# A norm's sums behind the next shared products, its square root one iteration later, and image loads in another order

## The chip, the cores and the metric

The kernel runs on one core of a Trainium2 chip. The metric is the device time of one execution in microseconds; several executions give a median and a range. Engines are written as in the profile: PE is TensorE, DVE is VectorE, ACT is ScalarE, POOL is GpSimd, SP is SyncE (here it only issues DMAs).

## The reference

Four residual layers act on x of shape (4, 32, 32, 16): batch, rows, columns, channels. Before each layer stands a group norm with 8 groups. Three layers are a convolution with a kernel of its own for every output pixel; the change lies in these. The fourth, a two-dimensional recursive filter done by Fourier transforms, is not touched.

```
def layer(v, M, W, G):                  # v = _gn(x)
    first   = einsum('ijpq,bpqc->bijc', M, v)
    shifted = conv3x3(v, K from G)       # for each output pixel (i, j): all (p, q), 16 channels
    diff    = relu(v[:, :, :, None, None, :] - shifted)
    second  = einsum('ijpq,bpqijc->bijc', W, diff)
    return first - second
x = x + layer(_gn(x), ...)               # three times

def _gn(v, G=8, eps=1e-5):               # mean and variance over rows, columns and the group's 2 channels
    return (g - m) / sqrt(s + eps)
```

## The kernel before, in words

**The tiles.** The 1024 output pixels of a layer make 128 blocks of 8 pixels by 16 channels, 128 rows of PE's output. One iteration is one block of one batch: PE makes shifted for all 1024 input pixels in a pair of PSUM banks (128 x 1024), and one DVE instruction (L771, 1.22 us) takes the min with zero, multiplies by W and sums along the row. There are 128 x 4 x 3 = 1536 iterations. `order` lists them, from `passes`: at a layer's ends the batches go in pairs, a = 0 (batches 0, 1) and a = 1 (batches 2, 3), so that one pair's norm runs beside the other pair's last blocks.

**One iteration** (`iteration`, L758 to L780). Four PSUM slots rotate. For iteration i PE holds, in its order, the six shared products of iteration i+1 (`shared_products`, L720: the products that two neighbouring pixels have in common, in half of the columns; ACT copies them into the other half, L729), then the own products of iteration i (`own_products`, L749: 16 matmul instructions in the trace, eight with f, the fp32 part of the image, and eight with n, its fp32r part). The products accumulate without a start flag onto columns that ACT has set to zero (`prepare`, L678, which for iteration i+2 is issued in the middle of the own products; `full` marks the slots whose columns were all written, so that this is allowed). The first 24 iterations go another way (`direct`, L701).

**What runs beside.** After each iteration `step()` advances a list of generators by one `yield`: first `todo` (norm, then store, then loads of a pair's image), then `tasks` (loads and splits of the taps, weights W). A `yield` thus is one iteration's distance, and what is issued between two of them takes its place in each engine's queue behind that iteration. The engines' queues are in the order of the program.

**The norm of a pair** (`group_norm`, L187). Row statistics on DVE, split into a high and a low fp32r piece (`in_pieces`); `piece_sums` (L155) adds them over partitions on PE with the matrix avg_r: a matmul with zeros over a whole bank (L165, start flag) and a small one with the pieces (L172), per half; ACT copies the result out (`held`, L181). The second sum is of the squared deviations; DVE then makes the variance v (L229), ACT its root r (L232), DVE refines r. Five norms of a pair go this way (two behind layer 0, two behind layer 1, one behind layer 2), with two sums each. The kernel's other norms use another sum.

**The image.** `store_image` (L401) makes the nine kinds of differences of the normed pair: POOL's subtractions L410, ACT's roundings L411 and L413, POOL's L417, edge copies on POOL (L420) and ACT (L421); then three DMAs on POOL's queue write them to `img` in DRAM (L423 to L425). Four iterations later `load_image` (L429) issues, per batch, 14 DMAs (L458) alternately on SP's and POOL's queue: six pieces of f (16 or 96 KB) and eight of n (72 KB). The second batch's follow three iterations behind the first's. SP's queue also carries the taps g (L588, 1536 KB), W (L634, 1024 KB) and F (L532); POOL splits the taps (L567, L569) and stores them to `gd` (L573).

Of the kernel before, what the change touches and what calls it, by code (L numbers as in the profile page):

```python
# [15 lines left out]
P = 128  # L16
# [21 lines left out]
def conv_stack_kernel(ctx, tc, x, M, W, raw_f, first_g, F, E, h0, coef, cst, dft, idp, idq, out):  # L38
    nc = tc.nc
# [15 lines left out]
    full, banks = [False] * 4, [0]  # L55

    def pair_psum(stays_full=False):
        slot = banks[0] % 4
        banks[0] += 1
        if not stays_full:  # L60
            full[slot] = False
        return ps.tile([P, 2, 512], F32, tag=f"pt{slot}", name="pt")

    def next_psum(stays_full=False):
        pt = pair_psum(stays_full)
        banks[0] -= 1
        return pt
# [14 lines left out]
    avg_r = const.tile([P, P], F32R, name="avg_r")  # L82
# [4 lines left out]
    nought_r = const.tile([P, 2], F32R, name="nought_r")  # L87
    nought = nought_r.bitcast(F32)[:, :1]
# [13 lines left out]
    start = [[range(layer * NBLK + lo, layer * NBLK + hi) for lo, hi in spans[layer]] for layer in range(3)]  # L102
# [20 lines left out]
    now = {"at": 0}  # L123
# [22 lines left out]
    def in_pieces(s):  # L146
# [5 lines left out]
        nc.vector.tensor_tensor(lo, s, hi.bitcast(F32), ALU.subtract)  # L152
        return pieces

    def piece_sums(pieces):  # L155

        pt = next_psum(True)  # L160
        nb, _, nw = pieces.shape[1:]
        n = nb * 4 * nw
        for h in range(2):
            rows = slice(64 * h, 64 * h + 64)
            nc.tensor.matmul(  # L165
                pt[:, h],
                lhsT=avg_r[rows],
                rhs=nought_r[rows].unsqueeze(1).to_broadcast([64, 256, 2]),
                start=True,
                stop=False,  # L170
            )
            nc.tensor.matmul(  # L172
                pt[:, h, :n],
                lhsT=avg_r[rows],
                rhs=pieces[rows].rearrange("p b k w -> p (b k w)"),
                start=False,
                stop=True,
            )
        full[banks[0] % 4] = True
        held = work.tile([P, 2, 16], F32, tag="yt", name="held")[:, :, :n]  # L180
        nc.scalar.copy(held, pt[:, :, :n])  # L181
        return held.rearrange("p h (b k w) -> p b w h k", k=4, w=nw), AX.XY

    def as_it_is(s):
        return s

    def group_norm(xt, operand=in_pieces, sums=piece_sums):  # L187


        nb = xt.shape[1]  # L190
        vec = lambda name, n=1: small.tile([P, 2 * B, n], F32, tag=name, name=name)[:, :out]

        st = small.tile([P, B, 2, 3], F32, tag="st", name="st")[:, :nb]
        for b in range(nb):
            nc.vector.bn_stats(st[:, b].rearrange("p e k -> p (e k)"), xt[:, b])
            if operand is in_pieces:
                yield
        to_add = operand(st[:, :, :, 1:])
        yield
        yield  # L200
        pm, axes = sums(to_add)
        spread = sums is piece_sums
        if spread:
            yield
        out = pm.shape[1]
        both = vec("both", 2)
        nc.vector.tensor_reduce(both, pm, axes, ALU.add)
        neg, within = both[:, :, 0], both[:, :, 1]
        d = vec("d", 2)[:, :nb]
        nc.vector.tensor_tensor(  # L210
            d, st[:, :, :, 1], neg[:, :nb].unsqueeze(2).to_broadcast([P, nb, 2]), ALU.add
        )
        if spread:
            yield
        nc.vector.tensor_tensor(d, d, d, ALU.mult)
        nc.vector.tensor_scalar(within, within, -1 / half_blks, 1e-5, ALU.mult, ALU.add)
        if spread:
            yield
        to_add = operand(d.unsqueeze(3))
        yield  # L220
        if not spread:
            yield
        pv, axes = sums(to_add)
        if spread:
            yield
        v = vec("v")
        nc.vector.tensor_reduce(v, pv, axes, ALU.add)
        v = v[:, :, 0]
        nc.vector.tensor_tensor(v, within, v, ALU.subtract)  # L229

        r, q, rstd = (vec(name)[:, :, 0] for name in ("r", "q", "rstd"))
        nc.scalar.activation(r, v, AF.Sqrt)  # L232
        yield
        nc.vector.reciprocal(q, r)
        nc.vector.scalar_tensor_tensor(q, q, 0.5, v, ALU.mult, ALU.mult)
        if spread:
            yield
        nc.vector.scalar_tensor_tensor(r, r, 0.5, q, ALU.mult, ALU.add)
        nc.vector.reciprocal(rstd, r)
        if spread:  # L240
            yield
        return neg, rstd
# [3 lines left out]
    def image_tiles(layer, b):  # L246
        tile = lambda name, d, *shape: imp.tile([P, *shape], d, tag=f"{name}{b}", name=f"{name}{b}")
        ims[layer, b] = [tile("f", F32, 4, 2, 64), tile("n", F32R, 6, 3, 64)]
# [180 lines left out]
    def load_image(layer, a, batches=(0, 1)):  # L429

        of = lambda t: t.rearrange("p l k m -> p l (k m)")
        for b in batches:
            moves = []
            image_tiles(layer, 2 * a + b)
            f, n = ims[layer, 2 * a + b]
            base, unit = SIZE * b, f.shape[3]
            for half in range(2):
                other = 2 if half == 0 else 0
                h, p = 64 * half, 4 * half

                def rows(p, n, kind, size):
                    return img[a][p : p + n, :, base + kind : base + kind + size].rearrange(
                        "p c x -> c p x"
                    )

                src = img[a][p : p + 1, :1, base : base + 2 * unit]
                src = bass.AP(src.tensor, src.offset, [[row, 3 * C], [C * row, 4], [1, 2 * unit]])
                moves.append((of(f)[h : h + 3 * C], src))
                slot = f[h + 3 * C : h + 4 * C]
                moves.append((slot[:, :, 0], rows(p + 1, 4, unit, unit)))  # L450
                moves.append((slot[:, :, 1], rows(p + other, 4, 2 * unit, unit)))
                for k in range(4):
                    piece = h + 32 * (k % 2) + 16 * (k // 2)
                    to = n[piece : piece + C].bitcast(F32)
                    moves.append((of(to), rows(p, 6, 3 * unit * (1 + k % 2), 3 * unit)))
            queues = nc.sync, nc.gpsimd
            for n, (to, src) in enumerate(moves):
                queues[n % len(queues)].dma_start(out=to, in_=src)  # L458
            for _ in range(3):
                yield  # L460
# [145 lines left out]
    for q in qs:  # L606
        load = max(0, done[-2] + 5, ready[q] - 20)
        at = load, max(ready[q], done[-1] + 1, load + (6 if q else 3))
# [48 lines left out]
    def is_shared(i):  # L657
        return order[i][2] > 2

    def prepare(i, rearm=False):  # L660

        if i in pts or i >= len(order):
            return
        slot = banks[0] % 4
        if is_shared(i) and not full[slot] and not rearm and is_shared(now["at"]) and i == now["at"] + 2:
            return
        pts[i] = pt = pair_psum(True)
        if is_shared(i):
            if not full[slot]:
                blk, b, _ = order[now["at"]]  # L670
                ni = ims[blk // NBLK, b][1].rearrange("p y k m -> p (y k m)")
                for half in range(2):
                    rows = slice(64 * half, 64 * half + 64)
                    nc.tensor.matmul(
                        pt[:, half], lhsT=avg_r[rows], rhs=ni[rows, :512], start=True, stop=True
                    )
            here = by_pixel(pt)[:, :, 0]
            nc.scalar.copy(here, nought.unsqueeze(2).to_broadcast(list(here.shape)))  # L678
        full[slot] = True
# [78 lines left out]
    def iteration(layer, acc):  # L758
        i = now["at"]
        blk, b, u = order[i]  # L760
        assert blk // NBLK == layer
        for j in range(i, i + 2):
            prepare(j)
        if full[banks[0] % 4]:
            prepare(i + 2)
        shared_products(i + 1)
        prepare(i + 2)
        pt = pts.pop(i)
        (own_products if is_shared(i) else direct)(u, blk, b, pt)
        junk = junkp.tile([P, S * S], F32, tag="junk", name="junk")  # L770
        nc.vector.scalar_tensor_tensor(  # L771
            junk,
            pt.rearrange("p h m -> p (h m)"),
            0.0,
            wts[w_at[i]][:, blk % 2, :],
            ALU.min,
            ALU.mult,
            accum_out=acc[b // 2][:, b % 2, blk % NBLK : blk % NBLK + 1],
        )
# [249 lines left out]
    held, last = (1, 7, 6, 0, 5), 2  # L1029
# [161 lines left out]
    pt = pair_psum()  # L1191
# [174 lines left out]
```

## Time and profile before

| | us |
| --- | --- |
| median of 3 executions | 2734.14 |
| lowest, highest | 2732.85, 2738.62 |
| the profiled execution | 2731.13 |
| its span | 2729.3 |
| PE's idle time in the three layers put down to ACT's L678 (8 times, longest 3.8) | 7.9 |
| the same put down to loads of g (2 times, longest 2.4) | 4.3 |

The span is the time between the first and the last instruction of the profiled execution; 1.8 us lie around it. The granted clock of PE was 0.999. In the timelines a row is: start in us from the span's beginning, length in us, engine, line of the kernel, operation, tiles written and read, shape, number of instructions drawn together; in brackets the idle time of the engine just before it and what ended that. PE's matmuls overlap in the records, so a stretch of PE is read from start to start.

### The profile page before, as it was taken

To read this page: it belongs to the slowest core of one execution; us is meant where nothing else is said; L and a number is where in the kernel's file an instruction comes from. 1 tells how busy PE (TensorE), PEld (TensorE's weight loads), DVE (VectorE), ACT (ScalarE), POOL (GpSimd) and SP (SyncE) were. 2 spreads that over 40 slices of the span, in tenths; PEclk is the share of its full clock that TensorE was granted. 3 is DMA by queue.
4 is the path that set the end of the run, shared out by engine and by line. 5 is a ranking of instruction groups with operands and counts; after the bars stand their busy time and mean duration, and the time that the engine had idled before them with its cause. 6 is when DMAs were issued, how large, how long until landed. Compare 5 with 4: busy or idle time off the path is not lost.

```text
span 2729.3 us, 81601 instructions
## 1 busy us (share of the span) xinstructions
PE 2704.5 (99%) x34450; PEld 2492.9 (91%) x34450; DVE 1941.3 (71%) x3246; ACT 1778.4 (65%) x3114; POOL 848.4 (31%) x1165
## 2 busy tenths in 40 slices
PE   8999999999999999999999999999999999999999
PEld 4998989999999999899999999999989999999995
DVE  5676867777777777677777777777767777777773
ACT  2666666666666666666666666666666666666661
POOL 6434455432312432422122221234232222232111
PEclk9999999999999999999999999999999999999999
DMA  8996577676674987656566766497866766676525
GB/s 293 313 345 208 190 245 247 227 250 232 234 274 180 328 240 294 219 224 242 206 244 227 259 218 274 176 328 238 323 205 228 262 219 253 230 248 239 226 84 86
DMA packets 134319, 652.14 MB, mean 239 GB/s; under 512 B 18864, under 2 KB 27328, under 8 KB 94912
## 3 DMA queue, kind: packets, MB, share of 16 engines
q1 hardware_dynamic: 84464, 473.63, 46.9%
q0 software_dynamic: 49056, 172.63, 19.8%
q8 instruction: 270, 4.42, 0.7%
q14 instruction: 97, 0.79, 0.1%
q10 hardware_dynamic: 432, 0.66, 0.1%
HBM read 487.24 MB, written 159.61 MB: 237 GB/s over the span
## 4 chain that ended last, share of the span: by engine, by line
PE 83%; DMA 2%; POOL 0%; DVE 0%; ACT 0%; SPq 0%; issue 0%; DVEq 0%; POOLq 0%
PE pt L749 64%; PE pt L720 17%; PE pt L1074 2%; DMA n<-img 1%; DMA img<-ye 1%; PE pt L492 1%; DMA f<-img 0%; SPq L458 0%; DVE junk L771 0%; ACT pt L678 0%; PE pt L894 0%; POOL ys L410 0%; PE pt L165 0%; POOL ys L417 0%; POOL ye L420 0%
## 5 line engine op out<-in xcount | busy, mean ns | idle before, releaser
L771 DVE SCALAR_TENSOR_TENSOR junk<-pt,w 128x1024 f32<-128x1024 f32 x1536 | 1879.8, 1224 | 740.4 <-PE pt L749 699.1
L749 PE MATMUL pt<-f,f 64*128 64x256 f32 x12096 | 1843.8, 376 | 0.0
L749 PE MATMUL pt<-n,g 64*128 64x256 f32 x12096 | 1817.7, 371 | 0.0
L749 PEld LDWEIGHTS pt<-n,g 64*128 64x128 f32 x12096 | 1210.2, 186 | 134.5
L678 ACT COPY pt<-nought_r 128x512 f32<-128x512 f32 x1512 | 888.7, 588 | 498.8 <-DVE junk L771 496.6
L729 ACT COPY pt<-pt 128x512 f32<-128x512 f32 x1512 | 860.8, 569 | 297.4 <-PE pt L720 296.8
L749 PEld LDWEIGHTS pt<-f,f 64*128 64x128 f32 x12096 | 985.6, 186 | 1.2
L720 PE MATMUL pt<-n,g 64*128 64x256 f32 x9072 | 817.8, 279 | 13.3 <-ACT pt L678 7.9
L720 PEld LDWEIGHTS pt<-n,g 64*128 64x128 f32 x9072 | 671.3, 185 | 23.4 <-ACT pt L678 12.3
L524 POOL TENSOR_TENSOR f<-f,cs 128x512 f32<-128x512 f32 x100 | 128.3, 1283 | 1177.9 <-DMA f<-in_F_dram 777.1
L563 POOL TENSOR_TENSOR raw<-raw 96x256 f32<-96x256 f32 x192 | 140.4, 731 | 7.6
L524 POOL TENSOR_TENSOR raw<-raw,cs 96x256 f32<-96x256 f32 x96 | 70.4, 734 | 205.6 <-DMA raw<-in_E_dram 205.4
L771 DVE DVE_READ_ACCUMULATOR junk<-pt,w 128x1 f32 x1536 | 126.6, 82 | 0.0
L569 POOL TENSOR_TENSOR raw<-raw,hi 96x512 fp32r<-96x512 f32 x96 | 123.0, 1281 | 7.1
L567 POOL CAST hi<-raw 96x512 fp32r<-96x512 f32 x96 | 58.4, 609 | 37.1 <-DMA gd<-hi 31.9
L573 POOL DMA_DIRECT2D gd<-hi x96 | 66.5, 692 | 0.3 <-issue 0.3
L573 POOL DMA_DIRECT2D gd<-raw x96 | 65.3, 681 | 0.6 <-issue 0.5
L508 POOL DMA_DIRECT2D fd<-ft x48 | 25.1, 532 | 88.2 <-ACT ft L500 87.7
L701 PE MATMUL pt<-first_f,f 64*128 64x512 f32 x192 | 48.0, 621 | 0.0
L410 POOL TENSOR_TENSOR ys<-y 128x64 f32<-128x64 f32 x36 | 9.5, 294 | 99.8 <-DVE y L381 99.8
L701 PEld LDWEIGHTS pt<-first_f,f 64*128 64x128 f32 x192 | 19.1, 195 | 18.6 <-issue 15.3
L458 POOL DMA_DIRECT2D n<-img x48 | 25.1, 527 | 11.1 <-DMA gd<-hi 9.3
(147 smaller groups left out, 409.6 us busy)
## 6 DMA issues: line engine op xcount, KB each, us to landing
w<-in_W_dram SPq DMA_DIRECT2D x199, 1024.0 KB, 11.5
g<-gd SPq DMA_DIRECT2D x100, 1536.0 KB, 10.1
gd<-hi POOLq DMA_DIRECT2D x96, 768.0 KB, 7.2
gd<-raw POOLq DMA_DIRECT2D x96, 768.0 KB, 8.9
f<-in_F_dram SPq DMA_DIRECT2D x100, 512.0 KB, 4.0
raw<-in_E_dram SPq DMA_DIRECT2D x96, 288.0 KB, 12.8
mt<-in_M_dram SPq DMA_DIRECT2D x12, 512.0 KB, 14.1
w<-in_M_dram SPq DMA_DIRECT2D x12, 512.0 KB, 17.2
```

The source lines that it names most:

```text
L524: engine.tensor_tensor(v, v, m.unsqueeze(1).to_broadcast([v.shape[0], v.shape[1], C]), ALU.subtract)
L563: nc.gpsimd.tensor_tensor(raw[:, 0], raw[:, 0], raw[:, k], ALU.add)
L567: nc.gpsimd.tensor_copy(hi, both)
L569: nc.gpsimd.tensor_tensor(lo, both, hi.bitcast(F32), ALU.subtract)
L573: nc.gpsimd.dma_start(out=gd[q % len(gd)][:, k].rearrange("a c n -> c a n"), in_=whole.unsqueeze(1).to_broadcast([96, 4, 4 * P]),)
L678: nc.scalar.copy(here, nought.unsqueeze(2).to_broadcast(list(here.shape)))
L701: nc.tensor.matmul(pt[:, half, px], lhsT=taps_of(u, blk, half, (0, 2)) if k == 2 else f[rows, k, at], rhs=rhs, start=k == 0, stop=k == 2,)
L720: nc.tensor.matmul(of_half(pt, half, 0), lhsT=taps_of(u, blk, half, (dy, dy), 0), rhs=ni[rows, dy : dy + 4, 2], start=False, stop=dy == 2, ...
L729: nc.scalar.copy(v[:, :, 1], v[:, :, 0])
L749: nc.tensor.matmul(of_half(pt, half, k), lhsT=w, rhs=rhs, start=False, stop=k == 1 and j == 2, skip_group_check=True,)
L771: nc.vector.scalar_tensor_tensor(junk, pt.rearrange("p h m -> p (h m)"), 0.0, wts[w_at[i]][:, blk % 2, :], ALU.min, ALU.mult, accum_out=ac ...
L1074: nc.tensor.matmul(rows.rearrange("n (j r) -> n j r", j=C)[:, :, 8 * cc :], lhsT=y(cc).rearrange("p q b -> p (q b)"), rhs=ts[k][q][:, :, : ...
```

## The change

- `piece_sums` no longer issues anything: it appends a function `sums` to a list `held_back`. The next iteration calls it between its shared products (of i+1) and its own products (of i).
- In `sums`, when the PSUM slot is marked full, ACT writes zeros into just the columns that the small matmuls will add to (`nc.scalar.copy(pt[:, :, :n], nought ...)`, n is 8 or 16 in each of two banks), and the two zero matmuls are left out.
- In such an iteration `prepare(i + 2)` is not called ahead of the sums; the condition in `prepare` is widened accordingly.
- `group_norm` has one more `yield` between the variance (DVE) and the root (ACT).
- `load_image` sorts its 14 moves: the eight n pieces first, the six f pieces behind.

```diff
+    held_back = []
+
     def piece_sums(pieces):
-        pt = next_psum(True)
         nb, _, nw = pieces.shape[1:]
         n = nb * 4 * nw
-        for h in range(2):
-            rows = slice(64 * h, 64 * h + 64)
-            nc.tensor.matmul(
-                pt[:, h],
-                lhsT=avg_r[rows],
-                rhs=nought_r[rows].unsqueeze(1).to_broadcast([64, 256, 2]),
-                start=True,
-                stop=False,
-            )
-            nc.tensor.matmul(
-                pt[:, h, :n],
...
-        full[banks[0] % 4] = True
         held = work.tile([P, 2, 16], F32, tag="yt", name="held")[:, :, :n]
-        nc.scalar.copy(held, pt[:, :, :n])
+
+        def sums():
+            marked = full[banks[0] % 4]
+            pt = next_psum(True)
+            if marked:
+                nc.scalar.copy(pt[:, :, :n], nought.unsqueeze(2).to_broadcast([P, 2, n]))
+            for h in range(2):
+                rows = slice(64 * h, 64 * h + 64)
+                if not marked:
+                    nc.tensor.matmul(
+                        pt[:, h],
+                        lhsT=avg_r[rows],
+                        rhs=nought_r[rows].unsqueeze(1).to_broadcast([64, 256, 2]),
+                        start=True,
+                        stop=False,
+                    )
+                nc.tensor.matmul(
+                    pt[:, h, :n],
+                    lhsT=avg_r[rows],
+                    rhs=pieces[rows].rearrange("p b k w -> p (b k w)"),
+                    start=False,
+                    stop=True,
+                    skip_group_check=marked,
+                )
+            full[banks[0] % 4] = True
+            nc.scalar.copy(held, pt[:, :, :n])
+
+        held_back.append(sums)
         return held.rearrange("p h (b k w) -> p b w h k", k=4, w=nw), AX.XY
...
         nc.vector.tensor_tensor(v, within, v, ALU.subtract)
+        if spread:
+            yield
...
         nc.scalar.activation(r, v, AF.Sqrt)
...
             queues = nc.sync, nc.gpsimd
+            moves.sort(key=lambda move: move[0].shape[1] == 4)
             for n, (to, src) in enumerate(moves):
                 queues[n % len(queues)].dma_start(out=to, in_=src)
...
         slot = banks[0] % 4
-        if is_shared(i) and not full[slot] and not rearm and is_shared(now["at"]) and i == now["at"] + 2:
+        if (held_back or not full[slot]) and not rearm and is_shared(now["at"]) and i == now["at"] + 2:
             return
...
         shared_products(i + 1)
-        prepare(i + 2)
+        if not held_back:
+            prepare(i + 2)
+        while held_back:
+            held_back.pop(0)()
+        if not is_shared(i):
+            prepare(i + 2)
         pt = pts.pop(i)
```

The instructions' new order in the queues, from the program as built: PE loses 20 zero matmuls, the 20 small ones move; ACT gains ten copies and has, in such an iteration, L729, the zero copy, the held copy, L678. On POOL, at the first and third of the five norms, L567 comes ahead of L410, and L569 between L410 and L417, where L567 was. On SP, at the same two norms, one load of W stands between the load of g and the second batch's seven image loads, where it was behind them.

More of the change, by code (lines that the diff above doesn't have):

```diff
@@ L153, in in_pieces @@
         return pieces
+    held_back = []
     def piece_sums(pieces):
-        pt = next_psum(True)
         nb, _, nw = pieces.shape[1:]
         n = nb * 4 * nw
-        for h in range(2):
-            rows = slice(64 * h, 64 * h + 64)
-            nc.tensor.matmul(
-                pt[:, h],
-                lhsT=avg_r[rows],
-                rhs=nought_r[rows].unsqueeze(1).to_broadcast([64, 256, 2]),
-                start=True,
-                stop=False,
-            )
-            nc.tensor.matmul(
-                pt[:, h, :n],
[L174 to L178, printed above, removed]
-        full[banks[0] % 4] = True
-        held = work.tile([P, 2, 16], F32, tag="yt", name="held")[:, :, :n]
-        nc.scalar.copy(held, pt[:, :, :n])
+        held = work.tile([P, 2, 16], F32, tag="yt", name="held")[:, :, :n]
+        def sums():
[24 more added lines that the diff above has]
+        held_back.append(sums)
         return held.rearrange("p h (b k w) -> p b w h k", k=4, w=nw), AX.XY
```

## The prediction, as put on record

> **What bounds the kernel now.** First the page's busy times and its chain: PE works for 2704.5 us of a span of 2729.3 us, and 83% of the chain that ended last is PE. No other engine is above 71%. So a stop of PE anywhere in the three layers is paid in full, and work taken off ACT, DVE or POOL counts only where it ends a wait of PE.
>
> ```profile
> PE 2704.5 (99%) x34450; PEld 2492.9 (91%) x34450; DVE 1941.3 (71%) x3246; ACT 1778.4 (65%) x3114; POOL 848.4 (31%) x1165
> ...
> PE 83%; DMA 2%; POOL 0%; DVE 0%; ACT 0%; SPq 0%; issue 0%; DVEq 0%; POOLq 0%
> ```
>
> Then PE's timeline around the first norm (rows: start, length, line, x count). A plain iteration is the distance between two bursts of L720: 868.43 to 870.12, 1.69 us. The sums of today (L165, L172) sit between two iterations.
>
> ```profile
> 868.43 0.52 PE L720 MATMUL pt<-n,g 64*128 64x256 f32 x6
> 868.79 0.60 PE L749 MATMUL pt<-f,f 64*128 64x256 f32 x4
> ...
> 870.12 0.52 PE L720 MATMUL pt<-n,g 64*128 64x256 f32 x6
> ...
> 871.82 0.38 PE L165 MATMUL pt<-nought_r,avg_r 64*128 64x512 f32 x2
> 872.03 0.17 PE L172 MATMUL pt<-pieces,avg_r 64*128 64x16 f32 x2
> 872.06 0.61 PE L720 MATMUL pt<-n,g 64*128 64x256 f32 x6
> ...
> 873.85 0.52 PE L720 MATMUL pt<-n,g 64*128 64x256 f32 x6
> ...
> 883.72 0.62 PE L720 MATMUL pt<-n,g 64*128 64x256 f32 x6 [0.69 <-ACT pt L678]
> ...
> 885.64 0.52 PE L720 MATMUL pt<-n,g 64*128 64x256 f32 x6
> ```
>
> One sum costs (872.06 - 870.12 - 1.69) + (873.85 - 872.06 - 1.69) = 0.25 + 0.10 = 0.35 us. Done at all ten sums in the same way, the excess is 4.2 us (eight between 0.32 and 0.45, one 0.56, one 0.74).
>
> The second stop, at 883.72, is the square root's. ACT's timeline shows it: L232 stands in ACT's queue 2.11 us early, waiting for VectorE's v, and the copy that zeroes the next products' columns (L678) stands behind it.
>
> ```profile
> 880.31 0.55 ACT L729 COPY pt<-pt 128x512 f32<-128x512 f32 x1
> 882.98 0.20 ACT L232 ACTIVATE r<-v 128x2 f32<-128x2 f32 x1 [2.11 <-DVE v L229]
> 883.09 0.58 ACT L678 COPY pt<-nought_r 128x512 f32<-128x512 f32 x1
> 883.60 0.55 ACT L729 COPY pt<-pt 128x512 f32<-128x512 f32 x1
> ```
>
> PE's previous burst began at 880.97, so this one is 2.75 - 1.69 = 1.06 us late, and the iteration that follows it takes 1.92 us (883.72 to 885.64), 0.23 more than a plain one. Counted instruction by instruction, all five norms show 1.28 to 1.30 us, 6.45 us together.
>
> **The sums, part by part.** The 20 matmuls L165 go. The 20 small L172 (10 sums) move: they now stand behind the next iteration's six shared products and ahead of this iteration's own products, in columns that a new ACT copy zeroes first. In ACT's queue this copy stands behind L729, and L729 waits for all six shared products. So the move adds a wait of PE on ACT, and queued behind it on PE are the 16 own products, for which VectorE and everything else wait. Its length, from the first shared product: L729 starts 0.61 us in (869.04 in ACT's rows, against 868.43); the next ACT instruction starts about 0.5 after a copy of this size (883.60 after 883.09); a copy of 32 columns takes 0.18 (the held copy L181, 180 ns); PE hears 0.05 later (883.72 after L678's end at 883.67). That is 1.34. The own products would have begun 0.36 in (868.79 against 868.43). PE stands still for 0.98 us. The two small matmuls add 0.1 (872.03 to 872.06, and a block longer by 0.09). For the start after the stop I take 0.2, from the 0.23 behind the 0.69 us gap. One sum: 1.28 us. Ten: 12.8, less the 4.2 of today: **+8.6**. Without the slower start it is 10.8, so +6.6; with the zero copy at 0.30 (the row of L413, a copy of 128 columns) it is 14.0, so +9.8. Nothing lies beside this wait, since PE is the engine that waits.
>
> [...]
>
> The held copy (L181, 0.18 us) and L678 then follow on ACT at about 1.5 and 1.7 us in and end by 2.3; the columns are wanted after 1.69 + 1.28 = 2.97. ACT is not late again.
>
> **The square root, one iteration later.** v is there 2.1 us after the root was queued; the root is now queued 1.69 us later and behind that iteration's copies, which bring it past 2.1. PE's five stops go: **-6.45** (at least -5.3, if only the 1.06 us at each goes and the slower iterations stay). Nothing is late in its place on PE, but centre, image store and image load come one iteration later.
>
> **POOL's order.** The tasks' instructions keep their iteration while the store moves, so at norms 1 and 3 the split of the taps changes place in POOL's queue: before the stores' second half (L417) stood the cast L567 (609 ns), now L569 (1281 ns). ACT's copies L421 wait for L417, L678 waits behind them, and PE for L678 (gaps 892.87 and on; the iterations of the four stores exceed 1.69 by 1.19, 0.55, 0.84 and 0.54 us). So 2 x 0.67 = **+1.3** (0, if the queue has room, to 1.4).
>
> **The image loads.** At norms 2 and 4 the last piece lands at 974.94 and 1854.47 and is used some 3.5 to 5 us later; 1.69 us fit in. At norms 1 and 3 nothing fits in: PE loses 0.66 us at 922.6 and 1.30 us around 1800 to 1802.7, waiting for n pieces and for g.
>
> ```profile
> 922.37 0.27 PE L720 MATMUL pt<-n,g 64*128 64x256 f32 x1
> 923.04 0.59 PE L720 MATMUL pt<-n,g 64*128 64x256 f32 x5 [0.40 <-DMA n<-img]
> ```
>
> The SyncE queue's timeline shows the loads of batch 1 of the pair, whose pieces those are:
>
> ```profile
> 909.29 0.37 SPq L588 DMA_DIRECT2D g<-gd  x1
> 910.04 2.17 SPq L458 DMA_DIRECT2D f<-img  x2
> 912.68 0.77 SPq L458 DMA_DIRECT2D n<-img  x2
> 913.50 0.43 SPq L458 DMA_DIRECT2D f<-img  x1
> 913.97 0.90 SPq L458 DMA_DIRECT2D n<-img  x2
> 919.41 0.35 SPq L634 DMA_DIRECT2D w<-in_W_dram  x1
> ```
>
> Their landings come in the order of issue: g at 919.35, then the seven pieces at 921.35, 921.57, ... 922.80. The DMA engines are full all the while (share 0.9 to 1.1 in each window of 3 us from 896 to 926; up to 414 GB/s). Three things act. n first brings the last n about 0.8 us forward (922.0), and f, wanted one iteration after n, is then last: at most -1.97 for both norms. The store one iteration later pushes the loads back by 0 (the engines had a backlog in any case) to 1.69 us. And, seen in the instructions' new order, SP now issues that w load (1 MB) between g and the seven pieces instead of behind them: 1 MB at 414 GB/s is 2.5 us, if the pieces queue behind it as they do behind g. For the 922.3 at which n is wanted this makes n late by 0 to 3.9 instead of 0.5 at norm 1, and much the same at norm 3: from -2 to +6 for both. I take **+3.5**: about 2.2 us late at each, because landings in the order of issue speak for the whole of w, and the full engines against the whole of the 1.69.
>
> Sum: 8.6 - 6.45 + 1.3 + 3.5 = +7. On the profiled execution's 2731.13 us that is 2738.1; the median of the runs, 2734.14, is 3.0 above it, so **2741**.
>
> **Rivals.**
> B, image loads worse. The pieces wait for w not 2.5 us but as long as w took from issue to landing, 919.41 to 925.00, 5.6 us. Two norms, 3.1 more each: 2741 + 6 = 2747. For it: the landings in a row; against it: that time was shared with other full queues. It decides where n lands more than 4 us after PE wants it.
> D, image loads cost nothing: the engines' backlog absorbs the later start, w comes in where others stand back, and n first saves half of its 1.97: 8.6 - 6.45 + 1.3 - 1 = +2.4, so 2736.5.
> A, not slower: PE does not pay the wait at the sums. The place is PE between L720 and L749; it decides whether the zero copy is done by the time the sixth shared product is issued. If it were, a sum would cost 0.1, so 1.0 in place of 4.2: -3.2 - 6.45 + 1.3 + 3.5 = -4.9, 2729; with D's image loads -9.4, 2725. Against it: the copy's place behind L729 in ACT's queue. For it: only that ACT's busy share is 65%.
> That the change does not do what it says (L172 still between zero matmuls where the columns were not marked) is out: in the built order all ten sums have their copy and none has L165.
>
> **Chances.** Main case 0.50, its own range 2736 to 2746 (sums +6.6 to +9.8, images +1 to +6); B 0.15; D 0.20; A 0.15. This kernel's measurement can tell about 0.2%, 5.5 us, from no change: faster is below 2728.7, slower above 2739.6. Faster: A with images, 0.10. Same: the rest of A 0.05, D 0.20 and the lower 0.15 of the main case: 0.40. Slower: 0.35 and B's 0.15: 0.50. The range that leaves out A's faster part and the end of B: 2731 to 2748.
>
> **What would show it.** Right: PE gaps of about 1 us between L720 and the sums with ACT's zero copy as the releaser, ten times; no gap before L720 after the root; ACT's root with no idle time on v; n<-img waits at norms 1 and 3 of 1 to 3 us. Wrong: sums' iterations near 1.8 us (A), n<-img waits gone (D) or over 4 us (B), or POOL's L417 no later than before.

## The result and the profile after

The changed kernel takes 2740.79 us (median of 12 executions, 2737.46 to 2745.47) beside 2732.59 us for the kernel before (12 executions, 2728.61 to 2738.62). The ratio is 1.0026 with a 95% interval of 1.0019 to 1.0034: 7.1 us slower (5.2 to 9.3); the two medians differ by 8.2 us. The profiled execution has a span of 2739.1 us, 9.8 more than before.

The page's busy times and chain say little by themselves. PE is as busy as before (2704.8 against 2704.5 us), although 20 matmuls are gone; the span grew by idle time.

```profile
PE 2704.8 (99%) x34430; PEld 2478.7 (90%) x34430; DVE 1942.9 (71%) x3246; ACT 1780.8 (65%) x3124; POOL 846.3 (31%) x1165
...
PE 84%; DMA 2%; ACT 0%; POOL 0%; SPq 0%; DVE 0%; issue 0%; DVEq 0%; ACTq 0%
```

PE's waits name it (engine, tile, line, releaser; total us, times, longest). Before, L720's waits on ACT's L678 stood on top with 7.9 us in 8 waits, and n<-img had 0.6.

```profile
PE pt L720 <- ACT pt L678: 7.9, 8, 3.8
...
PE pt L720 <- DMA n<-img: 0.6, 2, 0.4
```

After:

```profile
PE pt L178 <- ACT pt L167: 8.2, 10, 0.8
PE pt L731 <- ACT pt L689: 6.4, 3, 4.8
...
PE pt L731 <- DMA n<-img: 4.8, 2, 3.5
```

L178 is the small matmul of a sum (L172 before), L167 the new zero copy, L731, L740 and L689 are the former L720, L729 and L678, L760 the own products. The ten sums now wait for ACT every time, 0.82 us. The five waits at the root are gone (of the three left on L689, 4.8 us lies in the first 65 us). The image's wait has grown.

To compare place by place, I take the distance from one iteration's own products to the next on PE and subtract 1.69 us; what is left over is summed by its place:

| excess of the iterations, us | before | after | change | predicted |
| --- | --- | --- | --- | --- |
| ten sums | 4.2 | 12.2 | +7.9 | +8.6 |
| five roots | 6.45 | 0 | -6.45 | -6.45 |
| image stores (four norms) | 3.15 | 4.14 | +1.0 | +1.3 |
| image loads, first norm | 0.67 | 1.87 | +1.2 | together |
| image loads, third norm | 1.31 | 6.35 | +5.0 | +3.5 |
| sum | | | +8.7 | +7 |

Of the 1.1 us of the spans' difference that is left, about half lies in the first 115 us, where loads of g make PE wait for a time that differs from profile to profile; the other half is in no single place. I count neither to the change.

The table hides one thing. The shared and the own products are issued in pairs, one matmul for each half of the 128 rows (`half` in the kernel), and in a plain iteration the two of a pair start within 0.004 us of each other (877.464 and 877.468). In the kernel before, the sums leave one half behind the other: after the second sum of the first norm a pair starts at 880.969 and 881.179, 0.21 us apart, and the stop at the root brings the halves together again (883.718 and 883.721). The table goes by the half in front, and so counts this lag to the root. By the half behind, the ten sums before cost 5.0 us and the five roots 5.4; the sums' change is then +6.9 in place of +7.9, and the roots' -5.4 in place of -6.45. What the two come to together stays the same, +1.5 us.

PE's timeline at the first sum of the changed kernel (start, length, operation, count):

```profile
872.57 0.52 PE L731 MATMUL pt<-n,g 64*128 64x256 f32 x6
873.91 0.28 PE L178 MATMUL pt<-pieces,avg_r 64*128 64x16 f32 x2 [0.83 <-ACT pt L167]
874.05 0.68 PE L760 MATMUL pt<-f,f 64*128 64x256 f32 x4
...
875.47 0.52 PE L731 MATMUL pt<-n,g 64*128 64x256 f32 x6
```

ACT's timeline for the same time:

```profile
873.18 0.57 ACT L740 COPY pt<-pt 128x512 f32<-128x512 f32 x1 [1.12 <-PE pt L731]
873.66 0.20 ACT L167 COPY pt<-nought_r 128x32 f32<-128x32 f32 x1
874.29 0.18 ACT L187 COPY held<-pt 128x32 f32<-128x32 f32 x1 [0.43 <-PE pt L178]
```

The chain can be read off: six shared products, L740 behind them, the zero copy behind L740, and only then PE goes on, 1.34 us after the first shared product (873.91 - 872.57). This iteration takes 875.47 - 872.57 = 2.90 us, 1.21 more than a plain one.

At the third norm PE's timeline has the longest stop:

```profile
1805.03 0.59 PE L760 MATMUL pt<-n,g 64*128 64x256 f32 x4
1809.09 1.35 PE L731 MATMUL pt<-n,g 64*128 64x256 f32 x6 [3.47 <-DMA n<-img]
```

SyncE's queue there: the second batch's n pieces stand behind g and W. They land between 1808.59 and 1809.32, just behind W (1808.36; g landed at 1802.73).

```profile
1793.19 0.37 SPq L599 DMA_DIRECT2D g<-gd  x1
1793.66 0.39 SPq L645 DMA_DIRECT2D w<-in_W_dram  x1
1795.43 2.04 SPq L469 DMA_DIRECT2D n<-img  x4
1797.51 5.54 SPq L469 DMA_DIRECT2D f<-img  x3
```

### The profile page after: what moved, and what is told of

It reads as the page before. It is cut to its first block, busy times and chain, and to the rows that moved or that the text cites. A ratio compares the mean times of both kernels' runs of the same rounds, so it can differ in the third digit from the quotient of the medians.

```text
span 2739.1 us, 81579 instructions
## 1 busy us (share of the span) xinstructions
PE 2704.8 (99%) x34430; PEld 2478.7 (90%) x34430; DVE 1942.9 (71%) x3246; ACT 1780.8 (65%) x3124; POOL 846.3 (31%) x1165
## 4 chain that ended last, share of the span: by engine, by line
PE 84%; DMA 2%; ACT 0%; POOL 0%; SPq 0%; DVE 0%; issue 0%; DVEq 0%; ACTq 0%
PE pt L760 64%; PE pt L731 17%; PE pt L1090 2%; DMA n<-img 1%; PE pt L503 1%; DMA img<-ye 0%; ACT pt L740 0%; SPq L469 0%; PE pt L910 0%; DVE junk L787 0%; ACT pt L689 0%; POOL ys L427 0%; PE pt L178 0%; POOL raw L580 0%; POOL ye L430 0%
## 5 line engine op out<-in xcount | busy, mean ns | idle before, releaser
L760 PE MATMUL pt<-f,f 64*128 64x256 f32 x12096 | 1821.6, 376 | 0.0
L760 PE MATMUL pt<-n,g 64*128 64x256 f32 x12096 | 1793.3, 371 | 0.0
L760 PEld LDWEIGHTS pt<-n,g 64*128 64x128 f32 x12096 | 1175.4, 186 | 149.6
L689 ACT COPY pt<-nought_r 128x512 f32<-128x512 f32 x1512 | 887.9, 588 | 500.4 <-DVE junk L787 498.1
L740 ACT COPY pt<-pt 128x512 f32<-128x512 f32 x1512 | 860.9, 569 | 315.2 <-PE pt L731 314.6
L760 PEld LDWEIGHTS pt<-f,f 64*128 64x128 f32 x12096 | 954.0, 186 | 0.8
L731 PE MATMUL pt<-n,g 64*128 64x256 f32 x9072 | 802.0, 279 | 14.1 <-ACT pt L689 6.4
L731 PEld LDWEIGHTS pt<-n,g 64*128 64x128 f32 x9072 | 657.0, 186 | 22.9 <-issue 13.4
```

The source lines that it names most:

```text
L731: nc.tensor.matmul(of_half(pt, half, 0), lhsT=taps_of(u, blk, half, (dy, dy), 0), rhs=ni[rows, dy : dy + 4, 2], start=False, stop=dy == 2, ...
L740: nc.scalar.copy(v[:, :, 1], v[:, :, 0])
L760: nc.tensor.matmul(of_half(pt, half, k), lhsT=w, rhs=rhs, start=False, stop=k == 1 and j == 2, skip_group_check=True,)
```

## The experiments

All ratios are against the kernel before, measured beside it on the same chip; in brackets the 95% interval. A ratio's difference from 1 is turned into us with 2733.

**The root alone.**

```diff
         nc.vector.tensor_tensor(v, within, v, ALU.subtract)
+        if spread:
+            yield
```

> The kernel before with the one yield ahead of the root, nothing else. Theory (a sum of parts; the load of W that comes ahead of the second batch's image pieces holds them back as long as it takes to land, 4.6 and 5.6 us in the changed kernel's trace): the five stops at the root go, -6.45 us; POOL's order +1.0; the image waits at the first and third norm grow from 0.7 and 1.3 us to 4 and 7, since n is still loaded last and PE comes to them earlier: +9. In all +3.5 us against the kernel before (0 to +7). Rival (the load of W is no matter, the images come late only because the store is later): image waits +1.5 in all, total -4 us.

Measured: 1.0011 (1.0002 to 1.0021), +3.0 us. PE's waits show n<-img with 6.7 us in place of 0.6:

```profile
PE pt L722 <- DMA n<-img: 6.7, 3, 4.0
```

The roots' excess is 0; the image loads' is 3.3 and 8.9 us, against 0.67 and 1.31 (1.2 us of the 8.9 is a wait for g), and the stores' 4.1, by the half behind, against 3.1. The one yield takes away all five stops at the root and gives back more in the image loads. The rival's -4 us lies outside the interval.

**The sums alone.** The changed kernel without this yield and without the sort.

```diff
         nc.vector.tensor_tensor(v, within, v, ALU.subtract)
-        if spread:
-            yield
...
-            moves.sort(key=lambda move: move[0].shape[1] == 4)
```

> The kernel before with the sums behind the shared products and ACT's zero copies, without the later root and without the sorted loads. Theory (PE stands still for ACT at each sum): ten sums of 1.20 us in place of 0.42, +7.8 us; PE then comes later to the image pieces, so their waits of 0.7 and 1.3 us shrink by up to 1.6: in all +6 to +8 us, and the five stops at the root stay at 1.29 each. Rival (the sums cost PE little and the changed kernel is slower through its image loads): 0 to +2 us.

Measured: 1.0020 (1.0011 to 1.0030), +5.5 us. A sum has 1.19 to 1.31 us, image loads 1.6 us together. The stop at the root is 1.08 us here and not the 1.29 expected. That is no gain: by the half behind it was 1.08 before, too, and the other 0.21 is the lag that the old sums left. So the sums were expected 1 us too dear (+7.8; by the half behind, from 5.0 to 12.0, it is +6.9). The rival is out.

**The sort alone.**

```diff
             queues = nc.sync, nc.gpsimd
+            moves.sort(key=lambda move: move[0].shape[1] == 4)
```

> The kernel before with the sorted image loads alone. Theory: n lands about 0.8 us sooner at both norms, W stays behind the pieces; the waits of 0.7 and 1.3 us fall to 0 to 0.6 each: -1 to -2 us. Rival (f now comes last and PE waits for f in place of n): 0 us, with waits on f.

Measured: 0.9989 (0.9980 to 0.9999), -3.0 us. In the iterations only 1.2 us of it is found: the first norm's wait is gone, at the third 0.74 us is left, for which the profile names ACT's zeroing (g landed 0.35 us ahead of that burst). PE waits for no n there and for no f. The rest of the 3 us I can't place; it is inside the interval (-0.3 to -5.5 us).

**W behind the second batch's pieces.** The changed kernel, in which `load_image` sets a flag between its two batches.

```diff
+            between[0] = layer > 0 and b == batches[0]
             for _ in range(3):
                 yield
+            between[0] = False
...
-            while not w_free():
+            while between[0] or not w_free():
                 yield
```

> The changed kernel, with loads of W held back while an image's second batch is still to be issued, so that W stands behind these pieces on SP's queue as it did before the change. Theory (W ahead of them is what makes the pieces late): the waits for n of 1.9 us at the first norm and 6.3 us at the third (3.5 us of idling and two iterations at a lower clock) fall to 0 to 1 each: -6 us against the changed kernel (-5 to -8). Rival (the later start makes them late): -1 us at most, waits stay above 1.5 and 4 us.

Measured: 0.9995 (0.9985 to 1.0005), so some 8 us faster than the changed kernel. No wait for n or f is left at either norm (excess 0 at both, 8.2 us in the changed kernel); the store is as late as there. SyncE's queue at the third norm:

```profile
1789.19 0.37 SPq L603 DMA_DIRECT2D g<-gd  x1
1789.61 3.62 SPq L471 DMA_DIRECT2D n<-img  x4
1793.27 1.61 SPq L471 DMA_DIRECT2D f<-img  x3
1799.62 0.35 SPq L649 DMA_DIRECT2D w<-in_W_dram  x1
```

The pieces land from 1800.62 on, 1 us behind g (1799.56). So W's place makes the waits; the later start without it, with n first, costs nothing.

**The zero copy ahead of the shared products.** The changed kernel, with `sums` made a generator that yields behind the zero copy.

```diff
                 nc.scalar.copy(pt[:, :, :n], nought.unsqueeze(2).to_broadcast([P, 2, n]))
+            yield
...
+        for each in held_back:
+            next(each)
         shared_products(i + 1)
```

> The changed kernel, with the zero copy of a sum's columns issued ahead of the shared products, so that in ACT's queue it stands before L740 and not behind it. Theory (PE's 0.81 us gap at each sum is the wait for a copy that stands behind L740): the gaps close, a sum costs 0.2 to 0.35 us in place of 1.20, -9 us at the sums. PE then comes 1.8 us earlier to the image pieces, which still stand behind W: their waits grow by up to that at each norm, +2 to +4. In all -5 to -7 us against the changed kernel. Rival (PE would wait anyway, for the products' drain or for the held copy): the sums stay above 0.9 us, -2 us at most.

Measured: 1.0000 (0.9992 to 1.0009), 7 us faster than the changed kernel. The gaps of 0.82 us close; the ten sums come to 4.4 us in place of 12.2. But 0.44 a sum is more than the 0.2 to 0.35 expected, and little better than in the kernel before: 0.42 there by the half in front, 0.50 by the half behind (here 0.42 by the half behind). The image loads grow from 8.2 to 11.0 us, as PE comes earlier.

**Both repairs.**

> The changed kernel with both repairs: zero copy ahead of L740, W behind the second batch's pieces. Theory: sums -9, image waits -8, some 0.5 us of which come back because PE is earlier: -16 us against the changed kernel, -8 to -9 against the kernel before. Rival (the two repairs hide each other, and the image waits return when the sums get cheap): -3 us against the kernel before.

Measured: 0.9968 (0.9956 to 0.9981), 2724.88 us, -8.7 us. Image waits 0, sums 4.4 us. The repairs add up. PE's timeline shows what is left of a sum: the small matmuls take next to nothing (0.03 us, 870.54 to 870.57), but the next shared products begin 0.58 us after the last own block (872.15 against 871.57), where a plain iteration has 0.43, and the iteration after them is longer as well (1.79 us).

```profile
870.54 0.17 PE L179 MATMUL pt<-pieces,avg_r 64*128 64x16 f32 x2
870.57 0.68 PE L765 MATMUL pt<-f,f 64*128 64x256 f32 x4
...
871.57 0.58 PE L765 MATMUL pt<-n,g 64*128 64x256 f32 x4
872.15 0.62 PE L736 MATMUL pt<-n,g 64*128 64x256 f32 x6
```

ACT's timeline suggests why, and the last experiment tests it: the copy that zeroes their columns (L694) stands behind the zero copy, L745 and the held copy, and begins at 871.51.

```profile
870.80 0.57 ACT L745 COPY pt<-pt 128x512 f32<-128x512 f32 x1 [0.58 <-PE pt L179]
871.28 0.19 ACT L188 COPY held<-pt 128x32 f32<-128x32 f32 x1
871.51 1.11 ACT L694 COPY pt<-nought_r 128x512 f32<-128x512 f32 x2
```

**And POOL's order.** As above, with the split's second half held back while a store is in progress.

```diff
         nc.gpsimd.tensor_copy(hi, both)
         yield
+        while storing[0]:
+            yield
```

> As the run with both repairs, and the split's second half (L580 in the changed kernel) held on POOL until the image's store is issued. Theory (ACT's edge copies wait for POOL's second half, and PE behind them, 0.33 and 0.66 us more at the first and third norm than before): -1 us against the run with both repairs; the iterations at the store fall by 0.6 at each norm. The taps' store is an iteration later; its g has time, so nothing is late by it. Rival (the delayed taps make g late): +1 us or more, with waits on g.

Measured: 0.9967 (0.9954 to 0.9979), the same within the intervals. The stores' excess falls from 1.52 to 0.55 us at the first and third norm, more than expected; 1.4 us come back in the iterations at the image loads. So POOL's order is shown as the cause at the store; in the total its worth is not resolved, since the medians differ by 1.0 us (2724.88 and 2723.87), less than the intervals.

**The old sums.** The kernel before with later root, sort and W held back; the sums stay between the iterations.

> The kernel before with the later root, the sorted loads and W behind the second batch's pieces, but its own sums between the iterations. Theory: -6.45 at the root, +1.0 POOL's order, -2 image waits: -7.5 us against the kernel before, 1 to 2 us behind the run with both repairs, since a sum costs 0.42 and not 0.2 to 0.35. Rival (moving the sums is worth more than their own time, as it frees ACT and PE in other places): 4 us or more behind that run.

Measured: 0.9974 (0.9963 to 0.9985), -7.1 us. The distance to the run with both repairs is smaller than the intervals. In the iterations it is 0.7 us at the ten sums (4.9 against 4.2, by the half behind) and 1.4 us at the first norm's image loads, where PE still waits 1.0 us for n here. So moving the sums, even with the zero copy early, brings little by itself.

**Held copy and zeroing ahead of L751.** From the run with POOL's order, with ACT's queue in a sum's iteration rearranged.

```diff
+        between()
         v = by_pixel(pt)
         nc.scalar.copy(v[:, :, 1], v[:, :, 0])
...
+        def rest():
+            if held_back:
+                while held_back:
+                    next(held_back.pop(0), None)
+                prepare(i + 2, True)
+        shared_products(i + 1, rest)
```

> As the run with both repairs and POOL's order, and in a sum's iteration ACT's queue is: zero copy, held copy, zeroing for the iteration after next (L700), then L751; before it was zero copy, L751, held copy, L700. Theory (what is left of a sum's 0.44 us, of which the small matmuls are 0.1, is PE's next shared products waiting for L700, which stands behind L751 and the held copy): a sum falls to 0.1 to 0.2 us, -2.5 to -3.5 us against that run, -12 against the kernel before. Rival (the rest of the 0.44 is the change of weights and shapes on PE): no change, 0 to -0.5 us.

Measured: 0.9960 (0.9946 to 0.9973), 2721.97 us, -11 us. ACT's timeline now has the zeroing (L700) 0.46 us behind the start of the own products (869.96); above it was 0.94 (871.51 against 870.57):

```profile
870.21 0.18 ACT L188 COPY held<-pt 128x32 f32<-128x32 f32 x1 [0.59 <-PE pt L179]
870.42 0.59 ACT L700 COPY pt<-nought_r 128x512 f32<-128x512 f32 x1
870.95 0.55 ACT L752 COPY pt<-pt 128x512 f32<-128x512 f32 x1
```

A sum costs 0.08 us in seven of ten cases (0.16 to 0.31 in the others), 1.2 us in all; the span is 5.1 us shorter than that of the run with POOL's order. The medians differ by 1.9 us (2723.87 and 2721.97), and the intervals of the two ratios overlap, so the iterations show the gain at the sums and the total does not yet. At the first norm 1.0 us is still lost at the image loads (n<-img 0.6). This is the lowest median of the study.

## Why the prediction was right, and where it was not

The total was forecast at 2741 and +7 us; measured were 2740.79 and +7.1. The 2741 stood on a median before of 2734.14 us, from 3 executions; 12 executions gave 2732.59, and a distance between the medians of 8.2. So the agreement to 0.2 us is partly luck, and the parts are less exact, too.

- **The sums, right in mechanism.** The wait was predicted from L729's start, its length and the zero copy: 1.34 us from the first shared product on, which is what the trace shows, and 1.28 us a sum; measured 1.20, bounds 1.08 to 1.40. The part that was too big is the slower start: I took 0.2, and the iteration behind the 0.8 us gap is 0.09 longer. What the old sums cost was taken too low, 4.2 us for 5.0, because the lag between the two halves of the rows was read as the root's. The run with the zero copy ahead of L740 shows the cause: the gap goes when the copy is early.
- **The root, right that all of it goes.** All five stops are gone. 1.05 of their 6.45 us was the old sums' lag, which misprices the sums and the roots in opposite ways and nearly cancels in the total. The sign I named for it was not right: ACT's root still waits for v, 0.62 us at the first norm, but no PE instruction is late by it.

```profile
885.23 0.20 ACT L242 ACTIVATE r<-v 128x2 f32<-128x2 f32 x1 [0.62 <-DVE v L237]
885.34 0.58 ACT L689 COPY pt<-nought_r 128x512 f32<-128x512 f32 x1
```

- **POOL's order, right:** +1.0 for +1.3. POOL's timeline at the first norm has the split's second half in the store's way, where before it was the shorter cast, and the run with POOL's order takes it away.

```profile
891.94 0.60 POOL L567 CAST hi<-raw 96x512 fp32r<-96x512 f32 x1
892.51 0.31 POOL L417 TENSOR_TENSOR ys<-y,ys 128x64 f32<-128x64 f32 x1
```

After:

```profile
893.73 0.79 POOL L420 TENSOR_TENSOR ys<-y 128x64 f32<-128x64 f32 x3 [0.88 <-DVE y L391]
894.48 1.28 POOL L580 TENSOR_TENSOR raw<-raw,hi 96x512 fp32r<-96x512 f32 x1
895.71 0.33 POOL L427 TENSOR_TENSOR ys<-y,ys 128x64 f32<-128x64 f32 x1
```

- **The image loads, right in kind and wrong in size:** +6.2 for +3.5, just above the bound of +6. The mechanism, W in front of the pieces, was the one named, and W held back takes all of it away. The term that failed is "1 MB at 414 GB/s is 2.5 us": W landed 4.6 us (first norm) and 5.6 us (third) behind g. That is nearer to the 5.6 us of rival B than to 2.5. The taking of +3.5 was loose, too: "about 2.2 us late at each" is 4.4 us; less the 1.97 lost before that gives +2.4, and only less the 0.5 of lateness named for each norm does it come to +3.4. In the window from 1806 to 1809 the DMA engines were 46% busy and moved 75 GB/s, so W's last parts did not come at the 414 GB/s that the forecast took from the kernel before; what held them back was not shown. Against it, the later start cost less than half of the 1.69 allowed: at the first norm g landed at 919.76 against 919.35, while PE itself came to the image 1.4 us later than before (924.0 against 922.6). Thus the first norm stayed at +1.2.
- **A term that was missing:** the clock. Behind the 3.5 us stop the granted clock (the column before the DMA share) was 0.50, and the next two iterations were 1.5 and 0.6 us longer: 2.1 us of the 5.0 at the third norm.

```profile
1806.00:1809.00 3.00, 0.00 (x0) 0.00 (x0) 1.67 (x4) 0.00 (x0) 0.00 (x0) 0.77 0.46 75
1809.00:1812.00 3.00, 2.91 (x19) 2.85 (x20) 0.00 (x0) 1.08 (x2) 0.00 (x0) 0.50 0.86 289
```

So the agreement of the total owes something to chance: by the table the sums and POOL were 1.0 us too dear, the image loads 2.7 too cheap, and the sum over the iterations, +8.7, is 1.7 from the forecast. What decided the sign, the wait at ten sums and W ahead of the image, was predicted and is shown. Rival A's place was the right one to look at: with the zero copy early the wait is in fact gone; the changed kernel only puts that copy in the wrong place. What is left of a sum is then about 0.4 us, though, and not the 0.1 of rival A. Rival D is out, since the images did not come free.

## What to carry to other kernels

A few matmuls that are taken off the bounding engine are dear if what replaces them makes that engine wait for another (0.82 us at each sum here): look where the replacing instruction stands in the other engine's queue, put it ahead of the long one, and then look for what is late next. Moving a step by one iteration moves its DMAs past others in the same queue; list them and their sizes, and price a transfer ahead by the time between landings in the trace (4.6 and 5.6 us for W here), not by its bytes over the rate of one window (2.5 us at 414 GB/s). An edit that is slower alone (the root, +3.0 us) was 7 us faster with the loads sorted and W kept in its place, so look for what an edit sets loose before it is dropped.

## What the runs showed of the hardware that was not expected

The granted clock fell behind some stops of PE and held behind others that were as long or longer. It was granted at 0.50 behind stops of PE of 3.99 us (the root alone), 3.47 (changed kernel), 2.85 and 2.63 us (zero copy early, first and third norm), and 1.97 us (kernel before, at 108.7 us, where another stop of 2.4 us lay 16 us earlier). It held at 1.00 behind 2.49 us (the root alone, first norm), 2.69 (with POOL's order, at 109 us), 2.93 (the old sums, at 108 us) and 3.05 us (both repairs, at 107 us). Behind the gaps of 0.8 us at the sums it stayed at 1.00. The stops from 1.97 to 3.05 us fall on both sides, so in these traces the length of the stop alone does not decide.

The windows show one case of each kind (the first number behind the comma is PE's busy time in us, the third from the end the granted clock). In the kernel before the 1.97 us stop ends at 110.70, and in the window behind 111.40 the clock is 0.50:

```profile
107.99:111.40 3.41, 1.45 (x19) 1.27 (x17) 1.62 (x4) 0.67 (x2) 0.00 (x0) 1.00 0.92 354
111.40:114.82 3.42, 3.42 (x29) 3.42 (x25) 0.86 (x1) 1.30 (x3) 0.00 (x0) 0.50 1.05 428
```

With both repairs the stop of 3.05 us lies across the two windows, in which PE was busy for 1.63 and 2.15 us, and the clock held:

```profile
105.72:109.13 3.41, 1.63 (x21) 1.43 (x18) 2.47 (x4) 1.35 (x3) 0.00 (x0) 1.00 1.00 330
109.13:112.55 3.42, 2.15 (x28) 2.18 (x30) 0.01 (x1) 1.08 (x2) 0.00 (x0) 1.00 0.97 377
```

In the changed kernel the clock falls at 63.435, 111.222 and 1807.646 us, the last inside the stop of 3.47 us, and is back at 1.00 from 70.26, 114.64 and 1814.47 us on. What decides beside the length of a stop was not shown.
